# First batch of a two-layer adjacency kernel: edge tiles, turned copies, reciprocals and the head of the load queue

## The chip, the cores and the metric

The kernel runs on one core of a Trainium2 chip. The metric is the device time of one execution in microseconds; lower is better. Four engines compute: TensorE (PE, with its weight loads PEld), VectorE (DVE), ScalarE (ACT) and GpSimd (POOL). SyncE (SP) computes nothing; its queue issues most of the loads.

## The reference

Sixteen batches of N = 1024 nodes with D = 128 features go through two layers. Everything is float32.

```python
# layer 0
h = x @ Ww.T + Wb
e = (h @ A) @ h.T;  e = e + e.T
att = softmax(where(adj > 0, e, 0), axis=1) * adj
hp = relu(att @ h)
i, f, o = (sigmoid(hp @ w_u + x @ w_x) for each gate)
x1 = layernorm(x + o * tanh(i * hp + f * x))
# layer 1, four heads
h1 = x1 @ conv_w[hd] + conv_b[hd]
s = tanh(adj * (h1 @ attn_w[hd] @ h1.T))
out = layernorm(x1 + relu(relu(mean_over_heads(relu(s @ h1))) + x1))
```

The inputs x and adj also come turned, as xT and adjT.

## The kernel before

The work is in tiles of 128 rows. A batch has eight row blocks j. The order on each engine is the order in which the program writes the instructions; no scheduler moves them (`manual_schedule`). PSUM tiles that are named by `small` come from a pool of four buffers.

**Layer 0 of a batch** is cut into pieces with short names, and `run` writes them out in the order of a string: `L` loads a tile of adj, `E` makes its edge tile (adj > 0, `find_edges`), `Q` projects q, `H` and `h` make three groups of h on PE and DVE, `S` makes the scores of a row block j and lets ACT move them from PSUM into the big tile R with a bias from h, `T` turns the row's blocks and puts them into the column of R that mirrors them, `A` masks column j by its edge tile, takes its maximum and lets ACT do exp with the sum z (`mask`), `B` makes rz = 1/z and hz = h * rz and multiplies the column by adj (`weigh`); it then also issues the product of the row before into acc (`back`). After row 7 come `R` (relu), `P` (hp turned back, with the gates' sums), `G` (gates), `I`, `O`, `V`, `N` (inner part, outer part, layernorm in two halves).

R is symmetric before masking, so only the blocks on one side of the diagonal are computed. In the first batch PE turns the others through PSUM. Row 0 is turned by `turn_first_score` in two halves, and `place_first_score` (piece `t0`) copies both into R on DVE.

**Before the first piece** stand the small weights: A is made symmetric (`a_sym`), then `s_ww` = a_sym Ww, then `q_w` and the columns `c_col` and `sb_col`, the turned Ww (`wwT`), the broadcast bias (`wb_row`), and the gates' rows for x (`gate_x`), which are the last columns of the tile that `H` multiplies by. `keep_at_work(n)` issues n products of a zero tile.

**Queues.** SP issues xT, the eight adj tiles, x, the second batch's xT, the late weights, and the second batch's adj tiles. ACT issues A, Ww and Wb, POOL the three rows of x's gates. Each load from SP or ACT raises one of eight semaphores, and a later load that takes the same one waits for it on its queue. Edge tiles of the first batch are bfloat16 on DVE, but tiles 5 and 6 are on POOL; in all later batches they are on POOL.

**From the second half of layer 0 on**, pieces of the second batch are mixed in. The first batch's x1 is turned on PE in two halves (`turn_first_x1`) and then feeds layer 1: `head_uT`, `rows`, and 32 steps a batch of `layer1_step`, whose products fill PE while the next batch's layer 0 is done in between by the plans `BETWEEN`, `AHEAD` and `FIRST`.

Of the kernel before, what the change touches and what calls it, by code (L numbers as in the profile page):

```python
# [19 lines left out]
P = 128  # L20
# [4 lines left out]
def two_layer_adjacency_kernel(  # L25
# [19 lines left out]
    nc = tc.nc  # L45
    B, N, D = x.shape
    H = conv_w.shape[0]
    assert D == P and N % 512 == 0
    NB = N // P
    NH = N // 512  # L50
    BH = NB // NH
# [9 lines left out]
    def small(name):  # L61
        return ps_sc.tile([P, 512], F32, tag="sc", name=name)
# [4 lines left out]
    ones = sb.tile([1, P], F32, tag="u", name="ones", bufs=1)  # L67
    nc.vector.memset(ones, 1.0)
    ident = consts.tile([P, P], F32, name="ident")
# [4 lines left out]
    a_in = sb.tile([P, P], F32, tag="hz", name="a_in", bufs=4)  # L74
    nc.scalar.dma_start(a_in, A)
    ww_in = sb.tile([P, P], F32, tag="hz", name="ww_in", bufs=4)
    nc.scalar.dma_start(ww_in, Ww)
    wb_col = consts.tile([P, 1], F32, name="wb_col")

    wb_in = sb.tile([1, P], F32, tag="x1T", name="wb_in")  # L80
    nc.scalar.dma_start(wb_in, Wb.rearrange("(o d) -> o d", o=1))
    rows_x = sb.tile([3, P], F32, tag="s1", name="rows_x", bufs=4)
    for g, w in enumerate((wi_x, wf_x, wo_x)):
        nc.gpsimd.dma_start(rows_x[g : g + 1], w.rearrange("(o d) -> o d", o=1))
    rows_u = sb.tile([3, P], F32, tag="turn", name="rows_u", bufs=2)


    G = D + 4
    KG = 512 // G
    GROUPS = [range(k, min(k + KG, NB)) for k in range(0, NB, KG)]  # L90
# [4 lines left out]
    wb_row = consts.tile([P, G], F32, name="wb_row")  # L95
    nc.gpsimd.memset(wb_row[:, D:G], 0.0)
    gate_u, gate_x = ident_g[:, D : D + 3], wwT_g[:, D : D + 3]
# [32 lines left out]
    a_sym = sb.tile([P, P], F32, tag="hz", name="a_sym", bufs=4)  # L130
    s_ww = sb.tile([P, P], F32, tag="hz", name="s_ww", bufs=4)
# [8 lines left out]
    def keep_at_work(n):  # L140
        for _ in range(n):
            nc.tensor.matmul(idle[:, :P], warm[:, :P], warm[:, :P], start=True, stop=True)  # L142

    keep_at_work(7)
    pa, pb = small("p_a"), small("p_s")
    nc.tensor.transpose(pa[:, :P], a_in, ident)
    nc.vector.tensor_add(a_sym, pa[:, :P], a_in)
    keep_at_work(2)
    nc.tensor.matmul(pb[:, :P], a_sym, ww_in, start=True, stop=True)
    nc.vector.tensor_copy(s_ww, pb[:, :P])  # L150
    pc, pw = small("p_b"), small("p_ww")
    nc.tensor.transpose(pw[:, :P], ww_in, ident)
    nc.tensor.matmul(pc[:, P : P + 1], wb_in, ones[:, 0:1], start=True, stop=True)
    nc.tensor.matmul(pc[:, :P], ones, wb_in, start=True, stop=True)
    nc.vector.tensor_copy(wb_col, pc[:, P : P + 1])
    nc.scalar.copy(wwT, pw[:, :P])
    nc.scalar.copy(wb_row[:, :D], pc[:, :P])
    nc.gpsimd.tensor_copy(b_wide, wb_col.to_broadcast([P, P]))
    pq, pc = small("p_q"), small("p_c")
    nc.tensor.matmul(pq[:, :P], s_ww, ww_in, start=True, stop=True)  # L160
    nc.vector.tensor_copy(q_w, pq[:, :P])
    nc.tensor.matmul(pc[:, 0:1], s_ww, wb_col, start=True, stop=True)
    nc.tensor.matmul(pc[:, 1:2], a_sym, wb_col, start=True, stop=True)
    nc.vector.tensor_copy(c_col, pc[:, 0:1])
    nc.vector.tensor_copy(sb_col, pc[:, 1:2])
    keep_at_work(1)

    def finish_weights():
        pt = small("p_bsb")
        nc.tensor.matmul(pt[:, :1], b_wide, sb_col, start=True, stop=True)  # L170
        nc.tensor.matmul(pt[:, 1:4], rows_x, ident[:3, :3], start=True, stop=True)
        nc.vector.tensor_copy(wb_row[:, G - 1 : G], pt[:, :1])
        nc.vector.tensor_copy(gate_x, pt[:, 1:4])

    def turn_rows_u():
        pt = small("p_rows_u")
        nc.tensor.matmul(pt[:, :3], rows_u, ident[:3, :3], start=True, stop=True)
        nc.vector.tensor_copy(gate_u, pt[:, :3])
# [116 lines left out]
    def layer0(b):  # L295
# [5 lines left out]
        t = {}  # L301
# [85 lines left out]
        def turn_first_score(half):  # L387

            ls = range(max(half * BH, 1), (half + 1) * BH)
            t["turned", half] = ps = small(f"turn0_0_{half}")  # L390
            for i, l in enumerate(ls):
                nc.tensor.transpose(ps[:, ts(i, P)], t["R"][:, l, 0, :], ident)  # L392

        def place_first_score():
            for half in range(NH):
                ls = range(max(half * BH, 1), (half + 1) * BH)
                nc.vector.tensor_copy(
                    t["R"][:, 0, ls[0] : ls[-1] + 1, :],
                    t["turned", half][:, : len(ls) * P].rearrange("p (l d) -> p l d", d=P),
                )  # L400

        def find_edges(j):

            if b == 0:
                m = sb.tile([P, N], BF16, tag="h1", name=f"edge_{b}_{j}", bufs=NB + 1)
            else:
                m = sb.tile([P, N], U8, tag="edge", name=f"edge_{b}_{j}")
            engine = nc.vector if b == 0 and j not in (5, 6) else nc.gpsimd
            engine.tensor_scalar(m, adj_t[b, j], 0.0, None, ALU.is_gt)  # L409
            t["edge", j] = m.rearrange("p (k d) -> p k d", d=P)  # L410

# [13 lines left out]
        def weigh(j):  # L425

            s = t["R"][:, :, j, :]
            adj = adj_t[b, j].rearrange("p (k d) -> p k d", d=P)
            rz = sb.tile([P, 1], F32, tag="rz", name=f"rz_{b}_{j}", bufs=4)
            t["hz", j] = sb.tile([P, D], F32, tag="hz", name=f"hz_{b}_{j}", bufs=4)  # L430
            if (b, j) != (0, NB - 1):
                nc.vector.tensor_mul(s, s, adj)  # L432
            nc.vector.reciprocal(rz, t["z", j])
            if b == 0 and j >= NB - 2:
                nc.vector.tensor_scalar_mul(t["hz", j], t["h"][:, j, :D], rz)
            else:
                nc.scalar.mul(t["hz", j], t["h"][:, j, :D], rz)
            if (b, j) == (0, NB - 1):
                for ks in (ts(0, BH), ts(1, BH)):
                    nc.vector.tensor_mul(s[:, ks], s[:, ks], adj[:, ks])  # L440
            if j:
                back(j - 1)

# [15 lines left out]
        def rows_hp(groups):  # L459

            if groups[0] is GROUPS[0]:
                t["hp"] = sb.tile([P, NB, D + 3], F32, tag="hp", name=f"hp_{b}", bufs=1)
            for ks in groups:
                pt = small(f"pt0_{b}_{ks[0]}")[:, : len(ks) * (D + 3)]
                pt = pt.rearrange("p (k d) -> p k d", d=D + 3)
                for i, k in enumerate(ks):
                    nc.tensor.matmul(pt[:, i, :], t["hpT"][:, ts(k, P)], ident_g, start=True, stop=True)  # L467
                nc.scalar.copy(t["hp"][:, ks[0] : ks[-1] + 1, :], pt)
# [84 lines left out]
        def finish(p):  # L553
# [5 lines left out]
        pieces = {  # L559
            "W": load_xT, "X": load_x, "R": relu,  # L560
        }
        if b == 0:
            pieces.update(P=lambda: rows_hp(GROUPS), G=gates, t0=place_first_score)
            for q in range(NH):
                pieces[f"T0.{q}"] = partial(turn_first_score, q)
                pieces[f"S1.{q}"] = partial(score, 1, [q])
        else:
            pieces.update(P=turn_hp, Y=partial(weigh_hp, 1), F=gate_f, i=gate_i, o=gates_io)
# [21 lines left out]
    def run(pieces, names):  # L590
        for name in names.split():
            if name in pieces:
                pieces.pop(name)()
# [7 lines left out]
    def turn_first_x1(x1, q):  # L601
        if q == 0:
            x1T_t[0] = sb.tile([P, N], F32, tag="x1T", name="x1T_0")
        pt = small(f"pt1_{q}")
        for i in range(BH):
            nc.tensor.transpose(pt[:, ts(i, P)], x1[:, q * BH + i, 0:D], ident)  # L606
        nc.scalar.copy(x1T_t[0][:, ts(q, 512)], pt)  # L607
# [100 lines left out]


    first, second, join = layer0(0), layer0(1), join_weights()  # L710
    run(first, "W L0 L1 L2 L3 L4 L5 L6 L7 X")
    run(second, "W")
    load_late_weights()
    run(second, "L0 L1 L2 L3 L4 L5 L6 L7")
    run(first, "E0 Q0")
    keep_at_work(1)
    finish_weights()
    run(first, "H0 h0 E1 E2 E5 E6 S0 T0.0 S1.0 T0.1 S1.1 A0 t0 E3 T1 S2 A1 E4 H1 h1 B0 Q1 T2 S3 A2")
    run(first, "B1 H2 h2 T3 S4 A3 E7 B2")
    turn_rows_u()  # L720
    run(first, "T4 S5 A4 B3 T5 S6 A5 B4 T6 S7 A6")
    run(second, "Q0")
    run(first, "B5 A7")
    run(second, "H0")
# [10 lines left out]
    run(second, "H2 S1")  # L735
    run(first, "I1")
    next(join, None)
    run(second, "S2")
    run(first, "O0 V0 O1")
    run(second, "h2 S3 Q1")  # L740
    run(first, "N0")
    turn_first_x1(x1_t[0], 0)
    run(first, "V1 N1")
    head_uT(0, 0, [0])
    rows(0, range(0, 2))
# [56 lines left out]
    half, quarter, eighth, rest = (last_end(B - 1, k, k + n) for k, n in cuts)  # L802
# [55 lines left out]
```

## Time and profile before

| What | us |
|---|---|
| Median of 4 runs | 2418.16 (2416.14 to 2420.32) |
| The profiled execution | 2416.57 |
| Its span in the profile | 2414.5 |
| PE busy | 2402.0 (99%) |
| DVE busy | 1556.0 (64%) |
| ACT busy | 1074.0 (44%) |
| POOL busy | 611.6 (25%) |
| First score moved by ACT | 11.35 from the span's start |
| First product into acc of batch 0 | 23.66 |
| First uT product of layer 1 | 59.06 |

The granted clock of PE is full throughout. The page's first section gives busy time by engine; a slice row gives the same for a stretch; the chain of work is followed back from the last instruction through what released each step. A time such as 11.35 is a start in microseconds from the span's start, and `out<-in` names the tiles. `L416` is line 416 of the kernel before; in the changed kernel most lines stand 8 to 10 lower.

### The profile page before, as it was taken

The page shows a single profiled execution, that of the slowest core. Times are in us where ns is not written, and L with a number is a line of the kernel's source. Part 1 is how long each engine was busy: PE and PEld are TensorE (multiplying, and loading weights), DVE is VectorE, ACT ScalarE, POOL GpSimd, SP SyncE. Part 2 cuts the span into 40 slices and gives each one's busy share as a digit, 9 for nine tenths or more (in the row PEclk, how much of TensorE's full clock was granted, in tenths as well). Part 3 has the DMA queues.
Part 4 walks back from the last instruction along what each step waited for, and adds up shares of the span by engine and source line. Part 5 has one row for each costly group of instructions (what it writes and reads, how often), then busy time and mean ns, then how long its engine had stood idle before and what let it go on. Part 6 is the DMA issues. An engine that isn't in the chain of part 4 may idle for free.

```text
span 2414.5 us, 20226 instructions
## 1 busy us (share of the span) xinstructions
PE 2402.0 (99%) x5980; PEld 1096.7 (45%) x5980; DVE 1556.0 (64%) x3280; ACT 1074.0 (44%) x1505; POOL 611.6 (25%) x379
## 2 busy tenths in 40 slices
PE   9999999999999999999999999999999999999998
PEld 5444444444444444444444444444444444444444
DVE  7766666666667666676666665666666576666554
ACT  6544344453444534445344454444444344443333
POOL 2314131241312413123131231313214132141000
PEclk9999999999999999999999999999999999999999
DMA  4334151341514415143242422425234251341010
GB/s 180 79 74 126 34 133 43 87 122 42 133 41 96 107 49 126 48 108 89 60 115 55 115 74 70 105 61 122 62 72 113 51 131 53 79 117 31 18 27 9
DMA packets 473309, 196.71 MB, mean 81 GB/s; under 512 B 414443, under 2 KB 439279, under 8 KB 473200
## 3 DMA queue, kind: packets, MB, share of 16 engines
q1 hardware_dynamic: 454525, 128.70, 22.6%
q0 software_dynamic: 18384, 66.59, 9.2%
q8 instruction: 47, 0.77, 0.1%
q14 instruction: 63, 0.51, 0.1%
q10 hardware_dynamic: 290, 0.13, 0.0%
HBM read 135.86 MB, written 59.51 MB: 81 GB/s over the span
## 4 chain that ended last, share of the span: by engine, by line
PE 99%; DVE 1%; ACT 0%; issue 0%; POOLq 0%; DVEq 0%; ACTq 0%
PE sc L643 36%; PE acc L649 36%; PE acc L448 9%; PE sc L357 5%; PE pR L614 5%; PE pT_u L246 5%; PE pR_h L338 1%; PE pT_q L246 1%; DVE R L416 0%; PE idle L142 0%; PE acc_q L672 0%; DVE R L432 0%; PE pt L467 0%; DVE edge L409 0%; PE pt L606 0%
## 5 line engine op out<-in xcount | busy, mean ns | idle before, releaser
L644 DVE TENSOR_TENSOR s<-sc,adj 128x512 f32<-128x512 f32 x1008 | 685.6, 688 | 710.7 <-PE sc L643 689.6
L645 ACT ACTIVATE s<-s 128x1024 f32<-128x1024 f32 x504 | 533.2, 1058 | 1032.0 <-DVE s L644 1031.8
L643 PE MATMUL sc<-uT,x1T 128*128 128x512 f32 x2048 | 962.4, 592 | 0.0
L649 PE MATMUL acc<-s,h 128*128 128x512 f32 x2016 | 947.3, 592 | 0.0
L649 PEld LDWEIGHTS acc<-s,h 128*128 128x128 f32 x2016 | 380.5, 190 | 484.7 <-issue 476.3
L643 PEld LDWEIGHTS sc<-uT,x1T 128*128 128x128 f32 x2048 | 387.0, 190 | 469.8 <-issue 403.7
L409 POOL TENSOR_SCALAR edge<-adj 128x1024 uint8<-128x1024 f32 (+1 forms) x122 | 339.1, 2780 | 322.7 <-DVE top_None L416 314.2
L226 POOL TENSOR_TENSOR rs<-rs,mhalf 128x8 f32<-128x8 f32 (+3 forms) x36 | 55.1, 1531 | 948.7 <-DVE rs L225 948.7
L448 PE MATMUL acc<-R,hz 128*128 128x512 f32 x512 | 240.6, 593 | 0.1
L423 ACT ACTIVATE R<-R,nmax 128x1024 f32<-128x1024 f32 x128 | 146.9, 1148 | 74.9 <-DVE nmax L421 70.3
L416 DVE CUSTOM_DVE_ANT_0 R<-R,edge 128x1024 f32<-128x1024 f32 (+1 forms) x128 | 155.0, 1211 | 0.7 <-PE turn L392 0.5
L432 DVE TENSOR_TENSOR R<-R,adj 128x1024 f32<-128x1024 f32 x127 | 154.4, 1216 | 0.0
L448 PEld LDWEIGHTS acc<-R,hz 128*128 128x128 f32 x512 | 97.0, 190 | 122.3 <-issue 116.0
L357 PE MATMUL sc<-xT,qT 128*128 128x512 f32 (+3 forms) x384 | 145.4, 487 | 2.9 <-ACT qT L250 1.7
L360 ACT ACTIVATE R<-sc,h 128x512 f32<-128x512 f32 (+1 forms) x192 | 110.7, 579 | 52.7 <-PE sc L357 47.5
L480 POOL TENSOR_TENSOR x1T<-hp,wu_b 128x1024 f32<-128x1024 f32 x45 | 107.7, 2393 | 103.5 <-DVE hws L486 63.3
L246 PE MATMUL pT_u<-x1T,ms 128*128 128x512 f32 x256 | 120.6, 592 | 0.7 <-ACT x1T L607 0.7
L614 PE MATMUL pR<-cw,x1T 128*128 128x512 f32 x256 | 117.6, 598 | 0.0
L357 PEld LDWEIGHTS sc<-xT,qT 128*128 128x128 f32 x384 | 69.6, 190 | 72.4 <-issue 59.6
L312 POOL DMA_DIRECT2D adj<-in_adjT_dram x112 | 65.5, 585 | 92.5 <-DVE s L644 92.5
L667 DVE SCALAR_TENSOR_TENSOR sum<-acc,sum 128x512 f32<-128x512 f32 x95 | 61.3, 686 | 42.1 <-PE acc L649 42.1
L617 ACT COPY h<-pR 128x512 f32<-128x512 f32 x128 | 72.3, 592 | 28.3 <-PE pR L614 26.6
(149 smaller groups left out, 1137.0 us busy)
## 6 DMA issues: line engine op xcount, KB each, us to landing
adj<-in_adjT_dram POOLq DMA_DIRECT2D x112, 512.0 KB, 4.0
adj<-in_adjT_dram SPq DMA_DIRECT2D x16, 512.0 KB, 7.2
x<-in_x_dram SPq DMA_DIRECT2D x16, 512.0 KB, 5.3
xT<-in_xT_dram SPq DMA_DIRECT2D x15, 512.0 KB, 10.7
dram_hp<-turn_hp SPq DMA_DIRECT2D x15, 512.0 KB, 2.6
hp<-dram_hp SPq DMA_DIRECT2D x60, 128.0 KB, 3.3
dram_x<-turn_x SPq DMA_DIRECT2D x15, 512.0 KB, 3.0
x1T<-dram_x SPq DMA_DIRECT2D x60, 128.0 KB, 6.5
```

What stands on the lines that cost most here:

```text
L246: nc.tensor.matmul(ps, w, src[:, ts(q, 512)], start=True, stop=True)
L357: nc.tensor.matmul(ps[:, : at - lo], t["qT"][:, ts(j, P)], t["xT"][:, lo:at], start=True, stop=True)
L409: engine.tensor_scalar(m, adj_t[b, j], 0.0, None, ALU.is_gt)
L416: nc.vector.tensor_tensor_reduce(s[:, ks], s[:, ks], t["edge", j][:, ks], 1.0, nmax, ALU.mult, ALU.max, top)
L423: nc.scalar.activation(s, s, AF.Exp, bias=nmax, accum_out=t["z", j])
L432: nc.vector.tensor_mul(s, s, adj)
L448: nc.tensor.matmul(t["acc"][:, ts(q, 512)], t["hz", j], t["R"][:, ts(q, BH), j, :], start=(j == 0), stop=(j == NB - 1),)
L614: nc.tensor.matmul(ps, x1T_t[b][:, ts(k, P)], cw.rearrange("p h d -> p (h d)"), start=True, stop=True)
L643: nc.tensor.matmul(ps, x1T[:, ts(m, P)], uT[:, ts(q, 512)], start=True, stop=True)
L644: nc.vector.tensor_mul(s[:, ts(q, 512)], ps, adj[:, ts(q, 512)])
L645: nc.scalar.activation(s, s, AF.Tanh)
L649: nc.tensor.matmul(acc[:, ts(q, 512)], h1[:, ts(hd, D)], s[:, ts(q, 512)], start=(m == 0), stop=(m == NB - 1),)
```

## The change

The loads of Ww and Wb go to the head of SP's queue, and the three rows for x's gates go from POOL's queue to ACT's. The head of PE's work is put in another order: four idle products fewer, the turned Ww and the products with Wb ahead of s_ww, a_sym times the bias column ahead of q_w, and the x gate rows ahead of q. All edge tiles of the first batch are made on DVE; `E1` stands ahead of the first group of h, and `E5`, `E6` and `E7` stand later. ACT copies the turned first row into R, in `turn_first_score`; piece `t0` is gone. `weigh` makes rz and hz ahead of the product with adj. `Q1` of the first batch stands right after `A1`. Of the second batch, `h2` stands ahead of `S2`, and `Q1` after the first half of x1 is turned.

```diff
@@ -74,14 +74,14 @@
     a_in = sb.tile([P, P], F32, tag="hz", name="a_in", bufs=4)
     nc.scalar.dma_start(a_in, A)
     ww_in = sb.tile([P, P], F32, tag="hz", name="ww_in", bufs=4)
-    nc.scalar.dma_start(ww_in, Ww)
+    nc.sync.dma_start(ww_in, Ww)
     wb_col = consts.tile([P, 1], F32, name="wb_col")
 
     wb_in = sb.tile([1, P], F32, tag="x1T", name="wb_in")
-    nc.scalar.dma_start(wb_in, Wb.rearrange("(o d) -> o d", o=1))
+    nc.sync.dma_start(wb_in, Wb.rearrange("(o d) -> o d", o=1))
     rows_x = sb.tile([3, P], F32, tag="s1", name="rows_x", bufs=4)
     for g, w in enumerate((wi_x, wf_x, wo_x)):
-        nc.gpsimd.dma_start(rows_x[g : g + 1], w.rearrange("(o d) -> o d", o=1))
+        nc.scalar.dma_start(rows_x[g : g + 1], w.rearrange("(o d) -> o d", o=1))
     rows_u = sb.tile([3, P], F32, tag="turn", name="rows_u", bufs=2)
 
 
@@ -141,36 +141,34 @@
         for _ in range(n):
             nc.tensor.matmul(idle[:, :P], warm[:, :P], warm[:, :P], start=True, stop=True)
 
-    keep_at_work(7)
-    pa, pb = small("p_a"), small("p_s")
+    keep_at_work(6)
+    pa, pw, pb, ps = small("p_a"), small("p_ww"), small("p_b"), small("p_s")
     nc.tensor.transpose(pa[:, :P], a_in, ident)
     nc.vector.tensor_add(a_sym, pa[:, :P], a_in)
-    keep_at_work(2)
-    nc.tensor.matmul(pb[:, :P], a_sym, ww_in, start=True, stop=True)
-    nc.vector.tensor_copy(s_ww, pb[:, :P])
-    pc, pw = small("p_b"), small("p_ww")
     nc.tensor.transpose(pw[:, :P], ww_in, ident)
-    nc.tensor.matmul(pc[:, P : P + 1], wb_in, ones[:, 0:1], start=True, stop=True)
-    nc.tensor.matmul(pc[:, :P], ones, wb_in, start=True, stop=True)
-    nc.vector.tensor_copy(wb_col, pc[:, P : P + 1])
     nc.scalar.copy(wwT, pw[:, :P])
-    nc.scalar.copy(wb_row[:, :D], pc[:, :P])
+    nc.tensor.matmul(pb[:, P : P + 1], wb_in, ones[:, 0:1], start=True, stop=True)
+    nc.tensor.matmul(pb[:, :P], ones, wb_in, start=True, stop=True)
+    nc.vector.tensor_copy(wb_col, pb[:, P : P + 1])
+    nc.scalar.copy(wb_row[:, :D], pb[:, :P])
     nc.gpsimd.tensor_copy(b_wide, wb_col.to_broadcast([P, P]))
-    pq, pc = small("p_q"), small("p_c")
+    nc.tensor.matmul(ps[:, :P], a_sym, ww_in, start=True, stop=True)
+    nc.vector.tensor_copy(s_ww, ps[:, :P])
+    pc, pq, px = small("p_c"), small("p_q"), small("p_x")
+    nc.tensor.matmul(pc[:, 1:2], a_sym, wb_col, start=True, stop=True)
+    keep_at_work(1)
     nc.tensor.matmul(pq[:, :P], s_ww, ww_in, start=True, stop=True)
     nc.vector.tensor_copy(q_w, pq[:, :P])
     nc.tensor.matmul(pc[:, 0:1], s_ww, wb_col, start=True, stop=True)
-    nc.tensor.matmul(pc[:, 1:2], a_sym, wb_col, start=True, stop=True)
     nc.vector.tensor_copy(c_col, pc[:, 0:1])
     nc.vector.tensor_copy(sb_col, pc[:, 1:2])
-    keep_at_work(1)
+    nc.tensor.matmul(px[:, :3], rows_x, ident[:3, :3], start=True, stop=True)
+    nc.vector.tensor_copy(gate_x, px[:, :3])
 
     def finish_weights():
         pt = small("p_bsb")
         nc.tensor.matmul(pt[:, :1], b_wide, sb_col, start=True, stop=True)
-        nc.tensor.matmul(pt[:, 1:4], rows_x, ident[:3, :3], start=True, stop=True)
         nc.vector.tensor_copy(wb_row[:, G - 1 : G], pt[:, :1])
-        nc.vector.tensor_copy(gate_x, pt[:, 1:4])
 
     def turn_rows_u():
         pt = small("p_rows_u")
@@ -387,17 +385,13 @@
         def turn_first_score(half):
 
             ls = range(max(half * BH, 1), (half + 1) * BH)
-            t["turned", half] = ps = small(f"turn0_0_{half}")
+            ps = small(f"turn0_0_{half}")
             for i, l in enumerate(ls):
                 nc.tensor.transpose(ps[:, ts(i, P)], t["R"][:, l, 0, :], ident)
-
-        def place_first_score():
-            for half in range(NH):
-                ls = range(max(half * BH, 1), (half + 1) * BH)
-                nc.vector.tensor_copy(
-                    t["R"][:, 0, ls[0] : ls[-1] + 1, :],
-                    t["turned", half][:, : len(ls) * P].rearrange("p (l d) -> p l d", d=P),
-                )
+            nc.scalar.copy(
+                t["R"][:, 0, ls[0] : ls[-1] + 1, :],
+                ps[:, : len(ls) * P].rearrange("p (l d) -> p l d", d=P),
+            )
 
         def find_edges(j):
 
@@ -405,7 +399,7 @@
                 m = sb.tile([P, N], BF16, tag="h1", name=f"edge_{b}_{j}", bufs=NB + 1)
             else:
                 m = sb.tile([P, N], U8, tag="edge", name=f"edge_{b}_{j}")
-            engine = nc.vector if b == 0 and j not in (5, 6) else nc.gpsimd
+            engine = nc.gpsimd if b else nc.vector
             engine.tensor_scalar(m, adj_t[b, j], 0.0, None, ALU.is_gt)
             t["edge", j] = m.rearrange("p (k d) -> p k d", d=P)
 
@@ -428,16 +422,14 @@
             adj = adj_t[b, j].rearrange("p (k d) -> p k d", d=P)
             rz = sb.tile([P, 1], F32, tag="rz", name=f"rz_{b}_{j}", bufs=4)
             t["hz", j] = sb.tile([P, D], F32, tag="hz", name=f"hz_{b}_{j}", bufs=4)
-            if (b, j) != (0, NB - 1):
-                nc.vector.tensor_mul(s, s, adj)
             nc.vector.reciprocal(rz, t["z", j])
             if b == 0 and j >= NB - 2:
                 nc.vector.tensor_scalar_mul(t["hz", j], t["h"][:, j, :D], rz)
             else:
                 nc.scalar.mul(t["hz", j], t["h"][:, j, :D], rz)
-            if (b, j) == (0, NB - 1):
-                for ks in (ts(0, BH), ts(1, BH)):
-                    nc.vector.tensor_mul(s[:, ks], s[:, ks], adj[:, ks])
+
+            for ks in (ts(0, BH), ts(1, BH)) if (b, j) == (0, NB - 1) else [slice(NB)]:
+                nc.vector.tensor_mul(s[:, ks], s[:, ks], adj[:, ks])
             if j:
                 back(j - 1)
 
@@ -560,7 +552,7 @@
             "W": load_xT, "X": load_x, "R": relu,
         }
         if b == 0:
-            pieces.update(P=lambda: rows_hp(GROUPS), G=gates, t0=place_first_score)
+            pieces.update(P=lambda: rows_hp(GROUPS), G=gates)
             for q in range(NH):
                 pieces[f"T0.{q}"] = partial(turn_first_score, q)
                 pieces[f"S1.{q}"] = partial(score, 1, [q])
@@ -713,12 +705,11 @@
     load_late_weights()
     run(second, "L0 L1 L2 L3 L4 L5 L6 L7")
     run(first, "E0 Q0")
-    keep_at_work(1)
     finish_weights()
-    run(first, "H0 h0 E1 E2 E5 E6 S0 T0.0 S1.0 T0.1 S1.1 A0 t0 E3 T1 S2 A1 E4 H1 h1 B0 Q1 T2 S3 A2")
-    run(first, "B1 H2 h2 T3 S4 A3 E7 B2")
+    run(first, "E1 H0 h0 E2 S0 T0.0 S1.0 T0.1 S1.1 A0 E3 T1 S2 A1 Q1 E4 H1 h1 B0 T2 S3 A2 E5 B1")
+    run(first, "H2 h2 T3 S4 A3 E6 B2")
     turn_rows_u()
-    run(first, "T4 S5 A4 B3 T5 S6 A5 B4 T6 S7 A6")
+    run(first, "T4 S5 A4 E7 B3 T5 S6 A5 B4 T6 S7 A6")
     run(second, "Q0")
     run(first, "B5 A7")
     run(second, "H0")
@@ -735,11 +726,12 @@
     run(second, "H2 S1")
     run(first, "I1")
     next(join, None)
-    run(second, "S2")
+    run(second, "h2 S2")
     run(first, "O0 V0 O1")
-    run(second, "h2 S3 Q1")
+    run(second, "S3")
     run(first, "N0")
     turn_first_x1(x1_t[0], 0)
+    run(second, "Q1")
     run(first, "V1 N1")
     head_uT(0, 0, [0])
     rows(0, range(0, 2))
```

## The prediction

> **What bounds the kernel now.** I read the page's busy row first, then the busy time in slices of the first 70 us, then the chain of work in order of time, and last the timeline of the stretches that the chain names.
>
> ```profile
> PE 2402.0 (99%) x5980; PEld 1096.7 (45%) x5980; DVE 1556.0 (64%) x3280; ACT 1074.0 (44%) x1505; POOL 611.6 (25%) x379
> ```
>
> TensorE is busy 2402.0 of 2414.5 us. The waits on PE after 62 us add up to 1.6 us, so only the first batch's lead-in can give time. In the slices the columns are start:end, length, then busy us (instructions) of PE, PEld, DVE, ACT, POOL, the granted clock, DMA share, GB/s:
>
> ```profile
> 0.00:10.00 10.00, 8.44 (x46) 7.18 (x47) 2.38 (x11) 2.65 (x5) 3.31 (x15) 1.00 0.83 296
> 10.00:15.00 5.00, 4.79 (x21) 2.48 (x20) 3.59 (x8) 2.34 (x4) 1.98 (x1) 1.00 1.03 409
> 15.00:20.00 5.00, 4.09 (x21) 2.64 (x21) 4.96 (x9) 4.08 (x8) 4.41 (x2) 1.00 0.62 192
> 20.00:30.00 10.00, 7.79 (x29) 4.26 (x29) 7.99 (x18) 6.92 (x16) 0.00 (x0) 1.00 0.12 34
> 30.00:40.00 10.00, 9.92 (x32) 4.75 (x31) 9.71 (x19) 7.73 (x18) 0.00 (x0) 1.00 0.65 246
> 60.00:70.00 10.00, 10.00 (x27) 4.58 (x26) 5.03 (x8) 6.44 (x11) 5.85 (x3) 1.00 0.43 120
> ```
>
> Idle PE lies ahead of 30 us, plus 0.84 us in 50 to 60. From 15 to 20 us DVE has no gap while POOL runs. The timeline shows why, and the chain shows who pays:
>
> ```profile
> 13.02 6.39 POOL L409 TENSOR_SCALAR edge<-adj 128x1024 bf16<-128x1024 f32 x2 [6.11 <-DMA adj<-in_adjT_dram]
> 16.70 2.06 DVE L416 CUSTOM_DVE_ANT_0 R<-R,edge 128x1024 f32<-128x1024 f32 x1
> 18.87 1.08 DVE L409 TENSOR_SCALAR edge<-adj 128x1024 bf16<-128x1024 f32 x1
> 21.55 1.20 DVE L416 CUSTOM_DVE_ANT_0 R<-R,edge 128x1024 f32<-128x1024 f32 x1
> ```
>
> ```profile
> 20.43 1.13 DVE R L432
> 21.56 0.09 DVE rz L433
> 21.64 0.02 issue
> 21.67 0.40 ACT hz L437
> 22.07 0.58 ACT qT L250
> 22.65 0.04 issue
> 22.70 1.12 PE sc L357 x2
> 23.82 1.72 PE acc L448 x4
> ```
>
> The same mask costs 2.06 us beside a POOL edge tile and 1.20 alone. PE's second score of row 3 (22.70) waits for the second half of qT, which on ACT stands behind hz, which waits for rz behind a 1.13 us product. From 33.05 the chain stays on PE to 45.70; there DVE's last product ends at 42.61, so DVE is only half a microsecond from being the bound.
>
> **What the Trainium skill says.** "SBUF — State Buffer", section "SBUF: two separate sides", calls the port pair shared by VectorE and GpSimd an exclusive lock, and the loser blocks for a whole instruction. The trace agrees in kind: 2.06 against 1.20. "VectorE: DVE Perf Modes", section "The perf-mode tier table", gives fp32 tensor_scalar twice the rate of tensor_tensor; here a 1024-wide edge tile takes 0.68 and a product 1.22, while POOL needs 3.2 for the edge tile. "TensorE: Matmul & The Clock Gate", Part 1, says PE runs at half clock for its first 3.4 us or so of work; the idle products take 0.24 per pass until 4.39 (3.35/14) and then 0.11 (0.45/4).
>
> **Part by part.** Times are starts in this one execution; a pass of a 512-wide product is 0.43 on the chain.
>
> *Head of PE.* One idle product less ahead of p_a (2 x 0.24 = 0.48) and two less after it (0.45); but p_ww (0.11 to 0.24) and both p_b products (0.31+0.33) now stand ahead of p_s. So p_s stays near 5.1 (0.05 to 0.2 sooner). p_q no longer waits behind p_b: 6.37 becomes about 6.15, and q's first half starts about 7.3 for 7.55. After it, before spends 1.13 us (8.41 to 9.54) on an idle product, b's dot product, the x gate rows and two DVE copies. Now the x gate rows go ahead, while DVE copies q_w, and only b's 0.12 is left. H0 starts near 8.35 for 9.54: 1.2 gained. The rows' loads leave POOL for ACT's queue: three issues of about 0.45 ahead of the table load (1.28), which ends near 3.9; ACT's first copy is due after 4.5, so they cost nothing.
>
> *Loads.* Ww and Wb cost SP two issues, about 0.9, ahead of xT. More: all eight hardware semaphores are then taken by small loads and xT, so the first adj load waits for a_in. SP's waits show that kind of wait already:
>
> ```profile
> SPq L312 <- DMA a_in<-in_L_gnn_A_dram: 1.2, 1, 1.2
> ```
>
> There it held the fourth adj load, with three queued ahead; now nothing but xT (0.5 MB) is in flight. At about 400 GB/s it runs out near 4.2, while adj_0, issued near 3.7, brings bytes about 1.0 later (SP's first issue at 0.72, first bytes before 2.0). I take 0.6 us of delay for every adj tile; the bounds are 0 (a_in lands sooner, as xT no longer competes) and 1.5 (0.9 of issue and 0.6 of bubble). SP's waits put adj_1's landing at 7.83 now, hence 8.4. E1 now stands ahead of h0 on DVE: 8.4 to 9.1, and H0 ends near 9.2. At 0.6 it is just hidden; beyond that h0 slips one for one.
>
> So ACT's first R eviction goes from 11.35 to about 10.1.
>
> *Turned copies.* DVE loses 1.15 us (L397) behind nmax; ACT gains 0.46+0.59. Its waits for PE there are 0.42 and 0.72, which cover it. The first exp goes from 15.20 to 13.95.
>
> *Edges.* POOL's two (6.39) go; DVE takes on 2 x 0.6 (its back-to-back step) and loses the stretch: 2.06-1.20, 1.08-0.68, 1.07-0.69, together 1.64. The second mask starts after turn 1, near 14.85, and ends 16.05 for 18.76.
>
> *Reciprocals, q sooner.* rz ahead of the product frees each hz by 1.13 us. ACT then has exp 1 at 16.9, qT's second half at 18.05 (21.97 before), hz0 at 18.65. The waiting score goes from 22.70 to 18.75 and the first product into acc from 23.82 to 19.6: 4.2 gained.
>
> *What is late next.* DVE. From h's second group (17.7, after PE's H1) its queue has no wait: h and gate 1.0, product 0 1.2, six masks with nmax at 1.34, three edges 1.8, six products at 1.14, six rz and gate_u 0.6, two hz with their waits 0.6, the two halves 1.2: 21.3, ending 39.0 for 42.61. That is 3.6. PE then does its last back from 39.4 and ends acc near 41.2 for 45.02. I take 3.7; bounds 3.0 (mul6 holds back 6) and 4.2 (DVE keeps the whole lead). In this stretch the second batch's first xT, p_last and the wide weights landed long before (28 us at the latest), also 0.6 later.
>
> *The second batch's pieces.* h2 (0.43+0.18) leaves the place ahead of N0 for a 0.52 wait on tanh. POOL's pow ends at 56.56, so N0 starts 56.62 for 56.89. Q1's 0.86 moves from ahead of x1's transposes into the wait behind them (58.40 to 59.06); 0.2 of it may stick out. Gain 0.3, bounds 0.0 and 0.8. After that PE is gapless and carries the shift to the end.
>
> **Sum**: 3.7+0.3 = 4.0 us. The profiled execution took 2416.57 (span 2414.5 and 2.1 around it), so 2412.6; it lies 1.6 under the median 2418.16, whose runs spread from 2416.14 to 2420.32. Forecast for the median: **2414.2**. A measurement here can tell about 0.2%, 4.8 us, from no change; the gain is just under it.
>
> **Rivals.** *Whole lead kept* (0.30): DVE's three edges fall into waits (before, DVE waits 1.87 for h's third group at 26.03), so the lead of 4.2 reaches acc's end, and the tail gives 0.8: 5.0 to 5.5, 2413. For it: DVE is idle 2.0 us in 20 to 30. Against: after the change I find no wait left to fall into. *Late tiles* (0.12): adj 1.5 us later; E1 ends near 10.0, h0 slips 0.8, E2 and E3 follow: gain 2.0 to 3.0, 2415.7. For it: DMA is full (1.03) from 10 to 15. *Clock* (0.04), the side of a loss: with 7 idle products for 11 and a stop for a_in, the gate opens a window later. PE's work from 4.4 to 14 is about 8 us at full clock; each microsecond of it at half clock costs up to one. From 4 us of that on the gain is gone, from about 9 on the kernel is over 0.2% slower: 2423 or more. Against: PE has no gap over 0.5 us before H0 in either order. That an edit does nothing: the turned copies were covered by E3's own wait for turn 1 if PE is late there; then only 0.1 of the sum is lost.
>
> **Numbers.** Forecast 0.54 (own range 2412.6 to 2415.6 with the runs' spread), rivals as given. Of the forecast's share about a quarter (0.12) falls beyond 0.2% by the spread of medians. Faster 0.42, same 0.54 (with the late tiles), slower 0.04. Range 2411.6 to 2417.2.
>
> **What would show it.** Right: no POOL edge before 45 us; all DVE masks near 1.2; ACT's first L360-type eviction near 10.1; acc's first product near 19.6; DVE gapless from 18 to 39; PE's first uT product near 55.1 for 59.06. Wrong: E1 waiting for adj past 9.2, an idle DVE between masks, PE passes of 0.24 after 5 us, or a PE wait after 62 us that was not there.

## The result, and the profile after

The changed kernel takes 2415.7 us (median of 41 runs, 2413.3 to 2416.6), the kernel before 2417.92 (61 runs, 2415.5 to 2420.7). The ratio of the times is 0.9988, interval 0.9984 to 0.9992: about 2.9 us less, within the 0.2% that was called no difference. Forecast were 2414.2 and a gain of 4.0. The profiled execution of the changed kernel took 2416.24 (span 2414.4), that of the kernel before 2416.57.

The page's busy row, then the slices with the columns as before:

```profile
PE 2404.3 (100%) x5972; PEld 1098.5 (45%) x5972; DVE 1553.6 (64%) x3280; ACT 1064.9 (44%) x1507; POOL 603.5 (25%) x374
```

```profile
0.00:10.00 10.00, 8.96 (x32) 7.42 (x33) 2.33 (x10) 1.81 (x3) 1.59 (x12) 1.00 0.76 247
10.00:15.00 5.00, 5.00 (x18) 3.19 (x16) 2.00 (x5) 2.18 (x5) 0.00 (x0) 1.00 1.03 419
15.00:20.00 5.00, 4.44 (x20) 2.69 (x19) 3.81 (x10) 4.70 (x11) 0.00 (x0) 1.00 0.83 272
20.00:30.00 10.00, 9.88 (x42) 5.58 (x41) 9.20 (x20) 8.74 (x19) 0.00 (x0) 1.00 0.08 22
30.00:40.00 10.00, 9.41 (x30) 4.42 (x30) 9.82 (x22) 7.32 (x16) 0.00 (x0) 1.00 0.57 209
60.00:70.00 10.00, 10.00 (x27) 4.58 (x26) 5.27 (x9) 6.23 (x11) 5.43 (x2) 1.00 0.49 129
```

From 20 to 30 us PE rises from 7.79 to 9.88, as the forecast wanted. But PE is also busier ahead of 15 us (13.96 for 13.23) with fewer instructions (50 for 67). Work that takes longer with fewer instructions is a sign of the clock. The timeline of PE at the head shows it, first for the kernel before, then for the changed one (start, busy us, line, operation, count; `pT_q_first` is the first half of q, and the first `pR_h` is the piece `H0`):

```profile
7.39 1.02 PE L324 MATMUL pT_q_first<-xT,q_w 128*128 128x512 f32 x2
9.54 0.91 PE L338 MATMUL pR_h<-wwT_g,xT 128*128 128x132 f32 x6 [0.48 <-DVE wwT_g L173]
```

```profile
5.47 0.80 PE L155 MATMUL p_s<-ww_in,a_sym 128*128 128x128 f32 x2
8.21 2.08 PE L322 MATMUL pT_q_first<-xT,q_w 128*128 128x512 f32 x2
10.36 1.67 PE L336 MATMUL pR_h<-wwT_g,xT 128*128 128x132 f32 x6
```

The same product takes 2.08 for 1.02. The trace keeps its own record of the granted clock, which begins when the full clock opens: at 13.03 us in this execution, at 4.38 in that of the kernel before. Until then PE runs at half clock. The first eviction of R on ACT comes at 13.49, 2.1 later than before (11.35), and the last back products still end a little sooner (44.90 for 45.02). VectorE's timeline and the chain show where the lost 2.1 us came back:

```profile
18.30 1.22 DVE L410 CUSTOM_DVE_ANT_0 R<-R,edge 128x1024 f32<-128x1024 f32 x1 [0.76 <-PE turn L373]
19.64 0.68 DVE L403 TENSOR_SCALAR edge<-adj 128x1024 bf16<-128x1024 f32 x1
21.50 0.15 DVE L425 RECIPROCAL rz<-z 128x1 f32<-128x1 f32 x1
21.57 1.20 DVE L432 TENSOR_TENSOR R<-R,adj 128x1024 f32<-128x1024 f32 x1
22.69 1.22 DVE L410 CUSTOM_DVE_ANT_0 R<-R,edge 128x1024 f32<-128x1024 f32 x1
```

```profile
21.64 1.52 PE sc L355 x4
23.16 1.72 PE acc L440 x4
...
39.55 5.35 PE acc L440 x12
44.90 0.68 PE pR_h L336 x6
...
58.81 0.94 PE pT_u L244 x2
```

No mask of 2.06, edge tiles of 0.68, rz ahead of the product, and the scores of row 3 run into acc without the wait for qT. So the theory of the prediction stands for this stretch, and two things at the head are in question: the **clock**, and the **late adj tiles**. Their rivals were that VectorE's gapless stretch alone caps the gain, and that the two groups into which the times fall (2413.3 to 2414.3 in 17 runs, 2415.7 to 2416.6 in 24) have another cause.

Three marks make the profiles comparable: ACT's first eviction of R ("first R"); the end of acc, where the second batch's `pR_h` starts; and the first uT product. All profiles are in the table, those of the experiments below too. "Clock" is the opening of the full clock by the trace's record.

| Kernel | clock | first R | acc ends | R to end | end to uT | profiled run, us |
|---|---|---|---|---|---|---|
| before | 4.38 | 11.35 | 45.02 | 33.67 | 14.04 | 2416.57 |
| before, fewer idle products | 4.37 | 11.13 | 45.36 | 34.23 | 14.05 | 2416.84 |
| changed (first profile) | 13.03 | 13.49 | 44.90 | 31.41 | 13.91 | 2416.24 |
| changed (again) | 12.47 | 13.21 | 44.62 | 31.41 | 13.92 | 2415.89 |
| idle products as before | 4.41 | 11.22 | 42.63 | 31.41 | 13.92 | 2413.94 |
| 12 idle products | 4.11 | 11.19 | 42.60 | 31.41 | 13.92 | 2413.80 |
| h0 ahead of E1 | 4.45 | 10.09 | 41.49 | 31.40 | 13.91 | 2412.73 |
| h0 ahead, 2 idle products | 13.03 | 13.19 | 44.60 | 31.41 | 13.91 | 2415.79 |
| loads as before | 4.51, closed from 7.92 to 14.75 | 14.93 | 46.33 | 31.40 | 13.93 | 2417.54 |
| Ww and Wb as before | 13.18 | 14.05 | 45.46 | 31.41 | 13.92 | 2416.65 |
| rz and q as before | 4.80 | 11.57 | 44.08 | 32.51 | 13.92 | 2415.45 |
| edges on POOL | 11.99 | 12.97 | 44.06 | 31.09 | 13.92 | 2415.35 |
| turned copies on DVE | 13.88 | 13.77 | 45.20 | 31.43 | 13.92 | 2416.39 |
| second pieces as before | 13.44 | 13.69 | 45.10 | 31.41 | 14.04 | 2416.68 |

With either clock 31.40 or 31.41 us pass from the first R to the end of acc, in the changed kernel and in those that differ from it in the head alone. The kernel before is not so steady: 33.67 and, with fewer idle products, 34.23. There POOL's two edge tiles began later (13.67 for 13.02), and the second half of the first mask was stretched more. First the kernel before, then the one with fewer idle products:

```profile
13.85 1.07 DVE L416 CUSTOM_DVE_ANT_0 R<-R,edge,top 128x512 f32<-128x512 f32 x1 [0.36 <-PE turn L392]
```

```profile
13.63 1.63 DVE L415 CUSTOM_DVE_ANT_0 R<-R,edge,top 128x512 f32<-128x512 f32 x1 [0.36 <-PE turn L391]
```

### The profile page after: what moved, and what is told of

Same layout as the page of the kernel before. It is cut to its first block, busy times and chain, and to the rows that moved or that the text cites. A ratio compares the mean times of both kernels' runs of the same rounds, so it can differ in the third digit from the quotient of the medians.

```text
span 2414.4 us, 20157 instructions
## 1 busy us (share of the span) xinstructions
PE 2404.3 (100%) x5972; PEld 1098.5 (45%) x5972; DVE 1553.6 (64%) x3280; ACT 1064.9 (44%) x1507; POOL 603.5 (25%) x374
## 4 chain that ended last, share of the span: by engine, by line
PE 99%; DVE 1%; ACT 0%; issue 0%; POOL 0%; POOLq 0%; DVEq 0%; ACTq 0%
PE sc L635 36%; PE acc L641 36%; PE acc L440 9%; PE sc L355 5%; PE pR L606 5%; PE pT_u L244 5%; PE pR_h L336 1%; PE pT_q L244 1%; PE idle L142 0%; PE acc_q L664 0%; DVE R L410 0%; DVE u L528 0%; PE pt L459 0%; PE pT_q_first L322 0%; DVE st L219 0%
## 5 line engine op out<-in xcount | busy, mean ns | idle before, releaser
L403 POOL TENSOR_SCALAR edge<-adj 128x1024 uint8<-128x1024 f32 x120 | 332.7, 2772 | 316.6 <-DVE top_None L410 314.2
```

## The experiments

**Is it the clock?** First the changed kernel again (no edit).

> The changed kernel once more, for a second profiled execution. Theory (clock): the opening of the clock is drawn anew in each execution; the times again fall into a group near 2414 and one near 2416, and a profile from the lower group shows passes of 0.11 before 9 us, the one from the upper group again 0.24 up to about 13. Rival: the late clock is fixed by the order of the work; both groups of times have another cause, and the profile is as the first.

Median 2415.87 of 12; two runs at 2413.4 and 2413.7, ten from 2415.7 to 2416.5. The profile is of the upper group and has the late clock again (`pT_q_first` 2.08). With the first runs, 19 of 53 lie in the lower group; the groups' medians are 2413.91 and 2415.96. That the lower group has the early clock had to come from other kernels.

The idle products as before:

```diff
-    keep_at_work(6)
+    keep_at_work(7)
...
+    keep_at_work(2)
     nc.tensor.matmul(ps[:, :P], a_sym, ww_in, start=True, stop=True)
```

> The changed kernel with seven idle products at the head for six, and two more ahead of p_s, as the kernel before had them. Theory (clock): the strong idle products reach past 5 us again, so TensorE gets its full clock near 4.4 us (a pass of 0.11 in the second group of idle products, H0 near 0.91 long); H0 then starts near 8.8, the first exp near 14.5, and the median is 0.5 to 2 us below the changed kernel's, near 2414.5. Rival (path): the idle products only stand in the way; nothing is cold that matters, and the time is 0.3 to 0.9 us above the changed kernel's. Rival (adj tiles late): no change, since E1 and the masks wait for adj.

Median 2416.82 of 13, ratio to before 0.999 (0.9981 to 0.9998): five runs at 2413.72 in the middle, eight at 2417.50. The profile is of the lower group and has the early clock, H0 at 8.60 lasting 0.92. So the clock theory fits what the groups are, and is wrong that a few idle products decide them. Why the upper group lies 1.5 us above that of the changed kernel stays open. More idle products:

```diff
-    keep_at_work(6)
+    keep_at_work(12)
```

> The changed kernel with twelve idle products at the head for six. Theory (clock): passes of 0.24 until about 4.4 us and of 0.11 after, the group ends near 5.5, p_a starts 1.7 later than at 3.8, but everything after it is at full clock; the first product into acc comes at about 21 for 22.99, and the median is near 2414, with no runs in an upper group near 2416. Rival (path): the 1.7 us of the later p_a come out in the end, near 2417.5. Rival (adj tiles late or VectorE the bound): within 0.5 us of the changed kernel.

Median 2415.15 of 13, ratio 0.9988 (0.998 to 0.9996): six runs at 2413.97, one at 2415.2, six from 2416.3 to 2416.8. The upper group did not go away, and the later p_a (5.27) did not come out in the end: H0 starts 0.8 us later than in the kernel above (9.37 for 8.60), and yet ACT's first R comes at 11.19, as there (11.22). Something else set it. And the same cut in the kernel before, six idle products and none ahead of p_s:

```diff
-    keep_at_work(7)
+    keep_at_work(6)
...
-    keep_at_work(2)
     nc.tensor.matmul(pb[:, :P], a_sym, ww_in, start=True, stop=True)
```

> The kernel before with six idle products at the head for seven and none ahead of p_s: the idle products of the change alone. Theory (clock): the full clock comes only after 9 us, H0 lasts near 1.67 for 0.91 and ACT's first eviction of R comes 1.5 to 2 us later; the median rises by 1 to 2 us, to 2419 or 2420. Rival (path): PE's head gets 0.5 to 0.9 us shorter, and the median falls by as much, near 2417.2.

Median 2417.63 of 13, ratio 1.0001 (0.9993 to 1.0009): no change, and the profile has the early clock, where the theory forecast the late one. The times fall apart too, one at 2418.7, seven in 2416.0 to 2417.6 and five from 2420.0 to 2420.4; no profile of the upper ones shows whether they are the late clock. There is no sign that the cut of idle products is what the change lost by; 13 runs can't tell a small change in how often the clock comes late. The last test of the clock was two idle products, on the kernel with h0 ahead (below), whose groups are 2412.68 and 2416.06:

```diff
-    keep_at_work(6)
+    keep_at_work(2)
```

> The kernel with h0 ahead of E1, with two idle products at the head for six. Theory (clock): strong work on TensorE is too short for a whole window before 5 us whatever the phase, so the clock comes late (8 us or more) in every execution, the profile shows it, and no run lies in the lower group at 2412.3 to 2412.8: all are near 2416. Rival (the two groups have another cause, such as the transfers): the two groups stay, in like shares, since nothing on the path is taken away: p_a waits for a_in in any case.

Median 2415.79 of 13, ratio 0.9991 (0.9983 to 1.0): one run at 2414.6, all others from 2415.5 to 2416.6, none in the lower group. The timeline of PE:

```profile
7.62 2.08 PE L322 MATMUL pT_q_first<-xT,q_w 128*128 128x512 f32 x2
9.78 1.67 PE L336 MATMUL pR_h<-wwT_g,xT 128*128 128x132 f32 x6
11.24 2.77 PE L355 MATMUL sc<-xT,qT 128*128 128x512 f32 x4
```

p_a came 0.6 us sooner than with six, and everything behind it ran at half clock. That decides it: the groups are the clock. The full clock opens at 4.1 to 4.8 us or at 12.0 to 13.9, and wherever a kernel's times part into two, its profiled run with the late clock lies in the upper group, the one with the early clock in the lower.

The record says more of how it opens. In all profiles but one (the loads as before) the full clock lasts one stretch, of 2396.16, 2399.57, 2402.98 or 2406.40 us; in the one left it lasts 3.41 us, and then the clock is closed for 6.83. The long stretches are 702 to 705 times 3.413. The Trainium skill, "TensorE: Matmul & The Clock Gate", section "Part 1: The HAM clock gate (the "warmup" mystery)", gives just this window, free-running; the trace agrees in its length. Where the first window's end falls differs from execution to execution (the openings at 13.03 and 12.47 are of one kernel).

What opens the clock is not what the profile calls busy. Counted back from the opening at 13.03 in steps of 3.41 us, PE was busy for all of the windows from 2.79 to 6.20 and from 6.20 to 9.62, and the clock stayed at half. That the weak products between 4.4 and 8 us (one row or one column) do not count, so that a missed window costs two more, fits the openings, but was only argued.

**Are the adj tiles late?** In the profile with the idle products as before, the chain at the head is (start, us, what):

```profile
3.32 6.61 DMA adj<-in_adjT_dram
...
9.96 0.07 DVE edge L404
...
10.57 0.57 DVE h L341
11.18 0.05 issue
11.22 0.70 ACT R L359
```

E1 waits until adj_1 lands at 9.93, and h0 stands behind E1. H0 on PE was done 0.4 us before. So h0 was put ahead:

```diff
-    run(first, "E1 H0 h0 E2 S0 ...
+    run(first, "H0 h0 E1 E2 S0 ...
```

> The changed kernel with h's first group (h0) ahead of the second edge tile (E1) on VectorE. Theory (late adj and clock side by side): in executions where TensorE has its full clock by 5 us the head ends where adj_1 lands (9.93 in such a profile, for 8.4 predicted), so with h0 ahead ACT's first eviction of R comes near 9.8 to 10.2 for 11.2, VectorE's gapless stretch starts about 1 us sooner, and the lower group of times goes from 2413.9 to near 2413.0; executions with the late clock keep their 2416, because there H0 is later than adj_1. Rival (VectorE alone is the bound): no group moves by over 0.3 us. Rival (adj_2 and adj_3 late as well): the first exp waits for E1 or E3 instead, under 0.4 us is gained.

Median 2414.31 of 12, ratio 0.9984 (0.9976 to 0.9992). The lower group went from 2413.91 to 2412.68, the upper one stayed (2416.06 for 2415.96), both as the theory had them. The chain:

```profile
2.83 5.67 DMA adj<-in_adjT_dram
8.53 0.69 DVE edge L403
...
9.42 0.58 DVE h L340
...
10.09 0.70 ACT R L358
...
41.49 0.68 PE pR_h L336 x6
```

E1 is off the chain; now E0 and adj_0 stand on it. This is the version to keep, though its ratio to before is still within the 0.2%. The other side, the loads themselves, first all three as before:

```diff
-    nc.sync.dma_start(ww_in, Ww)
+    nc.scalar.dma_start(ww_in, Ww)
...
-    nc.sync.dma_start(wb_in, Wb.rearrange("(o d) -> o d", o=1))
+    nc.scalar.dma_start(wb_in, Wb.rearrange("(o d) -> o d", o=1))
...
-        nc.scalar.dma_start(rows_x[g : g + 1], ...
+        nc.gpsimd.dma_start(rows_x[g : g + 1], ...
```

> The changed kernel with Ww and Wb back on ScalarE's queue and the x gate rows back on GpSimd's. Theory (late adj): xT is the first thing on SyncE's queue again, adj's first load is issued near 1.6 for 2.9, adj_1 lands near 7.8 for 9.9, and where the clock is early the median of the lower group falls by about 1 us to 2413.0, as in the kernel with h0 ahead. Rival (the weights are the head): p_s and q's product wait for Ww and Wb, which come 0.5 us later, and the gain is lost: 2414 to 2415 in the lower group. Where the clock is late, no change.

Median 2417.32 of 13, ratio 0.9997 (0.9989 to 1.0005): the gain is gone, and neither theory had all 13 runs above 2416. PE's timeline and the slices say why:

```profile
8.89 0.55 PE L165 MATMUL p_x<-ident,rows_x 3*128 3x3 f32 x2 [1.63 <-DMA rows_x<-in_L_gnn_wo_x_dram]
```

```profile
5.00:10.00 5.00, 3.37 (x18) 2.87 (x19) 1.39 (x7) 0.53 (x2) 0.29 (x1) 0.79 1.00 351
10.00:15.00 5.00, 5.00 (x13) 2.98 (x12) 2.17 (x5) 0.91 (x3) 0.00 (x0) 0.52 1.02 413
```

The rows come late from POOL's queue, and p_x now stands ahead of q. PE idles 1.63 us, and the clock, open since 4.51, closes from 7.92 to 14.75 (0.79, then 0.52 in the slices). Only 0.66 us of the wait (7.26 to 7.92) lies ahead of the closing. In the window from 4.51 to 7.92 PE was busy for 2.38 of 3.41 us, part of it with weak products; in the kernel before with fewer idle products, 2.84 of 3.41 (7.78 to 11.20) left the clock open. How much is due to the wait and how much to the weak products was not separated. Moving the rows to ACT's queue is a condition of the new order, not a free extra. So Ww and Wb alone, the rows staying on ACT's queue:

```diff
-    nc.sync.dma_start(ww_in, Ww)
+    nc.scalar.dma_start(ww_in, Ww)
...
-    nc.sync.dma_start(wb_in, Wb.rearrange("(o d) -> o d", o=1))
+    nc.scalar.dma_start(wb_in, Wb.rearrange("(o d) -> o d", o=1))
```

> The changed kernel (E1 ahead of h0, as it is) with only Ww and Wb back on ScalarE's queue; the x gate rows stay behind them on that queue. This is the load part of the change alone undone, without the wait for the rows on GpSimd's queue that hid it in the kernel with all loads as before. Theory (late adj): adj's first load is issued near 1.6, adj_1 lands near 8, E1 no longer waits, p_s comes about 0.7 later (Ww lands near 4.85), H0 near 8.7 to 9.4, ACT's first eviction of R near 10.3 to 10.8 for 11.2, and the lower group of times lies 0.5 to 1.0 us lower than the changed kernel's 2413.9. Rival (adj is late because of the order on the DMA engines, not because of the two loads ahead): adj_1 still lands near 9.5 to 10, no gain. Rival (the weights are the head): the lower group is at or above 2414.

Median 2416.55 of 13, ratio 0.9997 (0.9989 to 1.0005); two runs at 2414.6 and 2414.8, the rest around 2416.65. The expected gain was wrong, and the rival that the weights are the head was right. The profile has the late clock; adj_1 lands at 8.89 for 10.00, but PE waits for A and Ww, and p_s comes at 6.44 for 5.47:

```profile
4.15 0.45 PE L146 MATMUL p_a<-ident,a_in 128*128 128x128 f32 x1 [0.18 <-DMA a_in<-in_L_gnn_A_dram]
4.89 0.47 PE L148 MATMUL p_ww<-ident,ww_in 128*128 128x128 f32 x1 [0.29 <-DMA ww_in<-in_L_gnn_Ww_dram]
```

Ww on SP's queue buys about 1 us at PE's head and pays with late adj tiles; with h0 ahead, only adj_0 and its edge tile are still on the chain.

**The parts behind the head.** Each was undone alone in the changed kernel.

Reciprocals and q (the old `weigh`, and `Q1` behind `B0`):

```diff
+            if (b, j) != (0, NB - 1):
+                nc.vector.tensor_mul(s, s, adj)
             nc.vector.reciprocal(rz, t["z", j])
...
-    run(first, "... A1 Q1 E4 H1 h1 B0 T2 ...
+    run(first, "... A1 E4 H1 h1 B0 Q1 T2 ...
```

> The changed kernel with the reciprocals and hz behind the products again and the second half of q (Q1) behind B0. If this part carries the gain, as the prediction's sum has it, the score of row 3 waits for qT's second half again, some 2.5 to 4 us of lead go, and the median is near 2418.5 to 2419. Rival (VectorE's gapless stretch, which does not care for the order inside it, sets the end): under 1 us lost, near 2416.5. Rival (mask and edges carry it): no change.

Median 2415.45 of 21, ratio 0.9991 (0.9984 to 0.9997). The overall median would say that nothing was lost, but 11 of its 21 runs drew the early clock. By groups it is 2415.07 for 2413.91 and 2417.51 for 2415.96: 1.2 to 1.6 us lost, less than the 2.5 to 4 that were expected and a little more than the rival's 1, and R to end is 32.51 for 31.41. The old wait is back in the chain, though shorter:

```profile
20.13 0.40 ACT hz L431
20.53 0.58 ACT qT L248
21.11 0.04 issue
21.16 1.12 PE sc L355 x2
22.28 1.72 PE acc L442 x4
```

Edge tiles 5 and 6 back on POOL, early:

```diff
-            engine = nc.gpsimd if b else nc.vector
+            engine = nc.vector if b == 0 and j not in (5, 6) else nc.gpsimd
...
-    run(first, "E1 H0 h0 E2 S0 ...
+    run(first, "E1 H0 h0 E2 E5 E6 S0 ...
```

> The changed kernel with the edge tiles 5 and 6 back on GpSimd, early. Prediction: the second or third mask lasts 2.06 for 1.22 and two edge tiles are stretched by 0.4 each, 1.6 us of VectorE's time, against 1.2 us of edge tiles that VectorE is spared: 0.4 to 1.5 us lost, near 2416.5 to 2417.3. Rival (VectorE is gapless from 18.7 on, so what it is spared counts in full, and the stretch falls into its gaps before): 0.5 to 1.2 us gained, near 2415.

Median 2415.8 of 21, ratio 0.9989 (0.9982 to 0.9995); groups 2413.61 and 2415.96. No loss; R to end is even 0.32 shorter (31.09). The timelines of POOL and of VectorE:

```profile
14.77 6.86 POOL L403 TENSOR_SCALAR edge<-adj 128x1024 bf16<-128x1024 f32 x2 [8.68 <-DMA adj<-in_adjT_dram]
```

```profile
15.47 1.07 DVE L410 CUSTOM_DVE_ANT_0 R<-R,edge,top 128x512 f32<-128x512 f32 x1 [0.36 <-PE turn L390]
...
17.78 1.22 DVE L410 CUSTOM_DVE_ANT_0 R<-R,edge 128x1024 f32<-128x1024 f32 x1 [0.44 <-PE turn L373]
...
19.12 1.33 DVE L403 TENSOR_SCALAR edge<-adj 128x1024 bf16<-128x1024 f32 x1
```

Stretched are the second half of the first mask (1.07 for 0.75) and one edge tile (1.33 for 0.68), together 0.97, while VectorE is spared two tiles of 0.6. The second mask, which took 2.06 before, keeps its 1.22, though it too lies beside POOL's tiles. And the stretch fell into waits, as the rival had it: the second mask waits 0.44 us for turn 1 where the changed kernel's waits 0.76, and the h behind the edge tile no longer waits the 0.69 that it did. The forecast of 0.4 to 1.5 us lost was wrong.

The turned copies on VectorE (`t0` behind `A0`):

```diff
-            nc.scalar.copy(
-                t["R"][:, 0, ls[0] : ls[-1] + 1, :],
...
-    run(first, "... T0.1 S1.1 A0 E3 ...
+    run(first, "... T0.1 S1.1 A0 t0 E3 ...
```

> The changed kernel with the first turned copies back on VectorE, behind the first mask and ahead of E3. Prediction: VectorE takes on 1.15 us and ScalarE loses 1.05; the second mask, which waits 0.76 us for turn 1 in the changed kernel, starts 0.3 to 0.4 us later, so each group of times (2413.9 with the early clock, 2416.0 with the late one) rises by 0.2 to 0.5. Rival (ScalarE was the later one: without its copies it gives R's rows and turn 1 sooner): no change or 0.3 us less. Rival (the whole 1.15 comes out, VectorE being gapless behind it): 1 us more.

Median 2416.01 of 21, ratio 0.9988 (0.9981 to 0.9994); groups 2413.67 and 2416.27; R to end 31.43. Nothing lost that the marks show: the copies took the place of the 0.76 us for which the second mask waits for turn 1, and the rest came out of the next wait, for h (0.49 for 0.69). This kernel and the next ran on another chip than the experiments above, so a few tenths between their groups and those above are not read.

The second batch's pieces:

```diff
-    run(second, "h2 S2")
+    run(second, "S2")
...
-    run(second, "S3")
+    run(second, "h2 S3 Q1")
```

> The changed kernel with the second batch's h2 and Q1 where the kernel before had them, ahead of N0 and of x1's transposes. The prediction put this part at 0.3 us (bounds 0 and 0.8): each group of times rises by 0.3, to 2414.2 and 2416.3. Rival (hidden): no change within 0.15. Rival (Q1's 0.86 counts in full): 0.8 more.

Median 2416.38 of 13, ratio 0.9992 (0.9983 to 1.0); one run at 2414.0, the others from 2416.1 to 2416.7 with a median of 2416.43. The end of acc to uT is 14.04 for 13.92: 0.12. The upper group's 0.5 (2416.43 for 2415.96) is no measure of it, since in the profile acc's end itself came later (45.10), with a later clock (13.44).

## Why the prediction was right or wrong

The range held, and so did the class that was given the most weight; the size did not: about 2.9 by the ratio, 2.2 by the medians, for 4.0. That the range held is in part luck: it was wide enough (2411.6 to 2417.2) for both groups of times, and on which of them the median falls is a matter of the draw. Taken by its own steps, against the kernel before with its early clock:

| Step | Forecast | With the early clock | With the late clock |
|---|---|---|---|
| Head, to the first R | 1.25 | 0.13 | -2.14 |
| First R to the end of acc | 2.45 | 2.26 | 2.26 |
| Second batch's pieces | 0.3 | 0.12 | 0.13 |
| Sum at the first uT product | 4.0 | 2.5 | 0.25 |

The early column is the kernel with the idle products as before, since no profile of the changed kernel itself drew the early clock; its lower group (2413.91) fits that profile (2413.94). The late column is the changed kernel's first profile. The second step is against the 33.67 of one profile; against the 34.23 of the kernel before with fewer idle products it is 2.82.

*Loads* is the term that was mis-sized: the delay was put at 0.6 us for every adj tile, at most 1.5, and adj_1 landed 2.1 us later (9.93 to 10.00 for 7.83). The first adj load was issued at 2.93 for 1.63, 0.8 of it for the two issues and 0.5 for the wait for A, which was foreseen. The estimate then netted this against the bytes still in flight. The transfer rates in slices of half a microsecond, of the kernel before and of the changed one, show what that missed:

```profile
GB/s 0 0 0 98 99 323 320 405 411 419 337 370 345 418 418 336 418 393 418 401 442 434 393 426 401 442 426 393 394 334 315 292 336 401 370 95 23 13 54 23
```

```profile
GB/s 0 0 0 69 196 94 250 369 333 132 184 336 336 385 369 393 385 352 418 336 426 393 451 393 418 434 418 418 410 426 377 355 333 319 354 346 304 179 112 44
```

From 1.5 to 6 us the changed kernel moves 0.41 MB less (the difference of the slices' sums, times 0.5 us), 1.0 us at 410 GB/s: a slower start besides the hole at 4.5 to 5.5. The rest of adj_1's delay is not settled. "E1 just hidden" fell with it, and ACT's first R came at 11.2 for 10.1. With h0 ahead of E1, the same forecast marks come out: 10.09 (forecast 10.1), first exp 13.94 (13.95), first acc product 19.75 (19.6), acc's end 41.49 (41.2), uT 55.40 (55.1), profiled run 2412.73 (2412.6). The *Late tiles* rival, given 0.12, is what the early executions show; its gain of 2.0 to 3.0 is what came with the early clock. That its 2415.7 is also the median measured is chance: that run lies in the group with the late clock. *Whole lead kept*, given 0.30, did not come: VectorE had no wait left in that stretch.

*Clock* was named, and dismissed with 0.04, on two grounds that fell. PE's having no gap did not save it: with the late clock PE is busy throughout from 5 to 10 us, and the clock stays at half. And it was treated as a thing that the change either does or does not do, where it is drawn in each execution, 34 of 53 times late here. Its price was right in kind and smaller than feared, 2.05 us between the groups. Whether the change made the late draw more frequent stays open: the times of the kernel before do not part cleanly enough to count, and the cut of idle products alone moved no median.

*Edges*, *Turned copies* and *Reciprocals, q sooner* were summed as a line of gains, and their sum at the end of acc was nearly right (2.26 for 2.45), as was the stretch without gaps (18.72 to 39.93 with twelve idle products, 21.2 for the 21.3 worked out). Their shares were not: undone alone, the reciprocals and q cost 1.1, the turned copies 0.02, the edges -0.32, together 0.8 of 2.26. About 1.5 us belong to none of them alone. The likeliest reason is that the parts cover for each other, but E7's later place was never undone, so this is not shown. The *Edges* step took the 2.06 for the price of any mask beside POOL's tiles; 0.97 was stretched in the new order, less than VectorE's own cost for two tiles.

## What to carry to other kernels

When a load is moved ahead of a stream of big loads, price the delay at the tile that an engine waits for, and look at what stands behind that wait in the engine's order; moving the waiting instruction back by one place was worth 1.2 us here in the executions that it could help. A gain of a few microseconds at a kernel's start has to be read by clock state: compare marks whose difference does not depend on the start, and medians within a group, since a median over both moves with the draw. Parts of a change that shorten the same stretch are not to be priced by their own sums.

## What the runs showed of the hardware

- The clock column says 1.00 for the first slices of nearly every profile, also where passes are at half speed; what is called a full clock throughout ahead of the prediction holds there only from 4.38 us on, and for 2406.40 us. Near the start the column falls only where the clock closes after it was open (0.79 and 0.52 with the loads as before). The pass durations show it, 0.24 against 0.11, and so does the record of the clock, which begins with the opening.
- PE busy for 5.00 of 5.00 us, from 5 to 10 us in the changed kernel, did not open the clock; in other executions it opened at 4.1 to 4.8 us, behind little more than idle products and transposes from 1.04 on.
- With the loads as before, a clock that had opened at 4.51 us closed at 7.92 for 6.83 us, 0.66 us into a wait of PE among weak products: it did not take a whole idle window of 3.41.
- A mask beside POOL's edge tiles took 2.06 us in the kernel before and 1.22 with the edges put back on POOL in the new order: lying side by side in time does not alone decide the stretch. In these two and in the kernel before with fewer idle products no instruction of VectorE was stretched by more than 0.9 us (half a mask of 1.63 for 0.75) beside POOL tiles of about 3 us and more. The mask of 2.06 (16.70 to 18.76) ended while POOL's second tile was still running (to 19.41), so the lock for a whole instruction that the prediction drew on is not what it shows.
- The median adj load took 5.1 us from issue to landing in the kernel before, and 6.2 in the changed one, where the first was issued 1.3 us later.
